# A graph network's prologue, reordered: the samples, the first window's indices and their transposes put ahead of the later layernorm chunks

## The chip, the cores and the metric

The kernel runs on one core of one Trainium2 chip. The metric is the device time of one execution in microseconds (us), the median over several runs. The five engines are named as in the profile: PE (TensorE; PEld is its weight load), DVE (VectorE), ACT (ScalarE), POOL (GpSimd) and SP (SyncE, which here issues transfers).

## The reference

Two message-passing layers on a graph of 6250 nodes with 64 features and 206250 directed edges (`src`, `dst`, sorted by `dst`). Each layer normalizes, aggregates over the edges, applies small dense layers, and is added to its input.

```python
h = jnp.maximum(_layernorm(x, axis=-1), 0.0)
x = x + gin(h)          # twice: h + segment_sum(h[src], dst), then relu(. @ Wa + ba) @ Wb + bb
h = jnp.maximum(_layernorm(x, axis=-1), 0.0)
x = x + message_net(h)  # y = mlp3(h[src]); z = segment_sum(y, dst); mlp3(concat([h, z]))
return x
```

## The kernel before

Instead of gathering per edge, the kernel builds the count matrix A (6250 by 6250, how many edges go from node to node) in 49 row tiles of 128 nodes and multiplies by it. A tile's counts are products of one-hot matrices. A is written to memory as bytes and read twice later, by two sweeps that make up the later part of the run; the first aggregation (`FirstSum`) uses each tile while it is still on chip.

**Finding the edges.** The edges of 256 nodes (a pair of tiles, number `q`) lie in a row in `dst`, so their start must be found. A sample of every 550th entry is loaded (`smp_i`), spread by a product with ones over all partitions (`smp_f`, `smp_d`, `smp`), and `search` counts on ACT with a Sign and an accumulated sum how many samples lie below a node; VectorE turns the count into `row` and `base` (L307, L308). `fetch_blocks` has GpSimd gather the block of 550 (`blk`, L316); `search_block` counts inside it (L327); `fetch_edges` makes the offsets (`off_f`, `off`, L336, L337) and has GpSimd gather the two index windows `d_win` and `s_win` (L341), 128 edges for each pair of nodes. All this goes in batches: batch 0 has one pair of tiles, the others two.

**From indices to counts.** `slots` turns a batch's windows on VectorE into three numbers per edge (L364 to L380); `cast` copies two of them on ACT to bf16; `turn` transposes the three on TensorE (L394) and copies them on ACT to `lkw` (L396). `hot` makes a tile's one-hots on VectorE: `there` (L405), `high` (L409) and `low` (L412); tile 0's come in three pieces (16, 16, 32), all other tiles' in one. `build` runs 64 small products per tile in four groups of 16 (L428), and ACT copies each group to int16 (`a`, L430). After each group a callback `between` runs: a quarter of the sum of the tile before (`FirstSum.quarter`, L571) and what the table `beside` holds for that place, slots, casts, turns, searches and fetches of later batches among them.

**The layernorm.** `values(t)` normalizes a chunk of 7 row tiles (`XT`; there are 7 chunks, 0 to 6). `norm` has VectorE sum (`mean`, L230), scale (L231), subtract (`xm`, L233), ACT square (`sq`, L235), VectorE sum the squares (`var`, L237), ACT take the root (L238), VectorE the reciprocal (L239) and the product `h` (L240). `split` then cuts `h` into three bf16 parts for the exact sum: ACT copies the first (L247), and two times TensorE subtracts what is there (an f32 product L250, one or two bf16 products L252) into the same pair of PSUM buffers `cnt` that the counts use, and ACT copies the rest (L253). The sum of tile 0 needs all seven chunks.

**What sets the order.** The instructions of an engine stand in an order that the framework's scheduler makes from the program's order, its data dependences and its own estimates. `behind(op, other)` adds an order without a semaphore: on the same engine `op` comes after `other`. Every engine works its list off in order, and a wait holds up all that stands behind it. Two buffers of one-hots (`hots`) and two pairs of `cnt` are in turn. In the program before, chunks 0 to 4, the searches of batches 0 to 3 and the fetches of batches 0 to 2 are written ahead of `build(0)`, chunks 5 and 6 behind it; chunks 0 and 1 are tied behind the samples. x is loaded in seven transfers, in turn on SP and ACT (`load_x`), SP's behind the samples.

Of the kernel before, what the change touches and what calls it, by code (L numbers as in the profile page):

```python
# [141 lines left out]
def load_x(nc, xs, x, engines):  # L142
    full = N // P
    nc.vector.memset(xs[:, full, :], 0.0)
    for i, t in enumerate(range(0, full, XT)):
        n = min(XT, full - t)
        engines[i % len(engines)].dma_start(xs[:, t:t + n, :], x[t * P:(t + n) * P].rearrange("(t p) d -> p t d", p=P))
    engines[0].dma_start(xs[:N - full * P, full, :], x[full * P:])


@with_exitstack
def fast(ctx: ExitStack, tc: tile.TileContext, x, src, dst, w, bad, out):
# [13 lines left out]
    def bank(name, dtype=FP):  # L166
        return pmix.tile([P, CH * 4 // mybir.dt.size(dtype)], dtype, tag="mix", name=name)


    root = const.tile([P, 1], FP, name="root")  # L170
# [4 lines left out]
    xs = const.tile([P, NT, D], FP, name="xs")  # L175
    load_x(nc, xs, x, [nc.sync, nc.scalar])
    w.load(nc.sync)
# [10 lines left out]
    ident_a = const.tile([P, P], BF, name="ident_a")  # L188
    nc.vector.tensor_scalar(ident_a, w.ident, 1.0 / UNIT, None, op0=OP.mult)
    word2 = once.tile([P, W, 2], BF, name="word2")  # L190
# [10 lines left out]
    smp_f = once.tile([SP_ROWS, SP_COLS], FP, name="smp_f")  # L201
    nc.vector.tensor_copy(smp_f, smp_i)
    nc.vector.memset(smp_f[0:1, 0:1], -1.0)
# [22 lines left out]
    def norm(to, t, n):  # L226

        xt = xs[:, t:t + n, :]
        mean = work.tile([P, n], FP, name="mean", tag=f"mean{n}")
        begun = nc.vector.tensor_reduce(mean, xt, axis=AX.X, op=OP.add)  # L230
        nc.vector.tensor_scalar_mul(mean, mean, 1.0 / D)  # L231
        xm = work.tile([P, n, D], FP, name="xm", tag=f"xm{n}")
        centered = nc.vector.tensor_tensor(xm, xt, mean[:, :, None].to_broadcast([P, n, D]), op=OP.subtract)  # L233
        sq = work.tile([P, n, D], FP, name="sq", tag=f"sq{n}", bufs=1)
        squared = nc.scalar.activation(sq, xm, AF.Square)  # L235
        var = work.tile([P, n], FP, name="var", tag=f"var{n}")
        nc.vector.tensor_reduce(var, sq, axis=AX.X, op=OP.add)  # L237
        nc.scalar.activation(var, var, AF.Sqrt, bias=w.eps, scale=1.0 / D)  # L238
        nc.vector.reciprocal(var, var)  # L239
        nc.vector.scalar_tensor_tensor(to, xm, 0.0, var[:, :, None].to_broadcast([P, n, D]), op0=OP.max, op1=OP.mult)  # L240
        return begun, centered, squared

    def split(parts, h):

        parts = [parts[:, :, i * D:(i + 1) * D] for i in range(NP)]
        banks = pcnt.tile([P, 2, CH], FP, name="cnt")[:, :, :h.shape[1] * D]
        nc.scalar.copy(parts[0], h)  # L247
        for i in range(2):
            ps = banks[:, i].rearrange("p (t d) -> p t d", d=D)
            nc.tensor.matmul(ps, w.ident, h, start=True, stop=False)  # L250
            for k in range(i + 1):
                nc.tensor.matmul(ps, minus, parts[k], start=False, stop=(k == i))  # L252
            nc.scalar.copy(parts[i + 1], ps)  # L253
# [22 lines left out]

    counted, swept = {}, []

    def behind(op, other):

        tc.add_manual_dep(op.ins, other.ins.name,
                          mybir.DependencyInfo(mybir.DependencyClass.NoSync, mybir.DependencyReason.DATA),
                          reason="order on an engine")
        return op

    def follow(op, engine):

        if engine in counted:
            behind(op, counted[engine])
# [57 lines left out]
    def slots(b):  # L347
# [31 lines left out]
        nc.vector.tensor_scalar(byte, byte, float(BYTE[1] - BYTE[0]), float(BYTE[0]), op0=OP.mult, op1=OP.add)  # L379
        nc.vector.tensor_tensor(byte, byte, shift, op=OP.logical_shift_left)  # L380
        numbers[b] = {0: word, 2: byte}
# [6 lines left out]
    def turn(b, i):  # L388
# [4 lines left out]
        for k in range(3):  # L393
            follow(nc.tensor.transpose(ps[:, k * P:(k + 1) * P], parts2[b % 2][:, i, k, :], identb), "PE")  # L394
        lkw = lkws[starts[b] + i] = wins.tile([P, 3, P], BF, name="lkw", bufs=5)
        nc.scalar.copy(lkw.rearrange("p a b -> p (a b)"), ps[:, :3 * P])  # L396

    def hot(lkw, g0, n):

        def of(i):  # L400
# [12 lines left out]
            low.rearrange("p (g i) w -> p g i w", i=2), there.rearrange("p g w i -> p g i w"),  # L413
            of(2)[:, :, :, None].to_broadcast([P, n // 2, 2, W]), op=OP.mult)
        return low.bitcast(F8), high

# [75 lines left out]
    def values(t):  # L492
        h = work.tile([P, XT, D], FP, name="h")
        begun, centered, squared = norm(h, t, XT)
        if t <= XT:
            behind(begun, sampled)
            behind(begun, bounds)
            behind(squared, searched[0])
        if t == XT:
            behind(centered, searched[1])  # L500
        split(hp[:, t:t + XT], h)
# [44 lines left out]
    values(2 * XT)  # L546
    search(2, op)
    fetch_blocks(2)
    values(3 * XT)
    search(3)  # L550
    fetch_blocks(3)
    values(4 * XT)
    for i in range(2):
        search_block(2, i)
    fetch_edges(2)

# [474 lines left out]
```

## Time and profile before

| what | before |
|---|---|
| median of 3 runs | 888.5 us (888.29 to 891.24) |
| profiled execution, its own time | 887.79 us |
| its span, from the first instruction to the last | 885.3 us |
| PE busy, share of the span | 854.7 us, 97% |
| DVE busy | 629.3 us, 71% |
| ACT busy | 570.7 us, 64% |
| chain that ended last, by engine | PE 81%, DVE 7%, DMA 5%, ACT 4% |

The profile is one execution. Its parts are the busy share of each engine in 40 slices of the span (a digit is tenths), the chain of waits followed back from the last instruction, groups of instructions by line, and, from the trace, a timeline (start, length, engine, line, operation, output and inputs, how often; in brackets the idle time before it and what ended that). Times in it are us from the span's start. Instructions of one engine overlap a little, so the time from one start to the next is some 0.07 us less on VectorE than the length shown. An L250 of the program is two rows in the trace.

### The profile page before, as it was taken

The numbers are of one execution on the slowest core, as the hardware profiler recorded it, in microseconds if no ns is written. First come the engines' busy times: TensorE is split into PE (matmuls) and PEld (weight loads), VectorE is DVE, ScalarE is ACT, GpSimd is POOL, SyncE is SP. The second block draws the span as 40 slices with busy tenths as digits, with TensorE's granted clock in tenths as the row PEclk, the third lists the DMA queues.
The fourth block names the chain that finished last, engine by engine and source line by source line (L and its number), as shares of the span: only waits on it lengthen the run. The fifth ranks groups of instructions, "written<-read, shape, count | busy, mean of one in ns | idle before, by whom it ended". The sixth has DMA issues, their size and how long they took to land.

```text
span 885.3 us, 19697 instructions
## 1 busy us (share of the span) xinstructions
PE 854.7 (97%) x8251; PEld 731.4 (83%) x8251; DVE 629.3 (71%) x933; ACT 570.7 (64%) x775; POOL 126.3 (14%) x86
## 2 busy tenths in 40 slices
PE   3899999999999999999999999999999999999996
PEld 1489999999999999887888887888889877776785
DVE  6999999999999998545555454555456767776662
ACT  5876777776777666645555555554545678777773
POOL 4547742424430200000000000000000000000000
PEclk9999999999999999999999999999999999999998
DMA  6335443335443323744544444444435688888881
GB/s 147 112 115 182 158 173 139 136 136 185 148 156 140 124 111 144 208 111 125 131 122 123 129 117 128 124 117 127 122 98 143 168 220 237 227 234 210 235 215 56
DMA packets 192086, 133.57 MB, mean 151 GB/s; under 512 B 34964, under 2 KB 183316, under 8 KB 191988
## 3 DMA queue, kind: packets, MB, share of 16 engines
q1 hardware_dynamic: 185544, 121.19, 46.6%
q0 software_dynamic: 3600, 10.32, 4.3%
q8 instruction: 66, 1.08, 0.5%
q10 hardware_dynamic: 2844, 0.72, 0.4%
q14 instruction: 32, 0.26, 0.1%
HBM read 91.25 MB, written 40.94 MB: 149 GB/s over the span
## 4 chain that ended last, share of the span: by engine, by line
PE 81%; DVE 7%; DMA 5%; ACT 4%; issue 1%; SPq 0%; ACTq 0%; DVEq 0%
PE acc L748 39%; PE acc L571 21%; PE cnt L428 8%; PE ps_t L450 5%; DMA a<-A 4%; PE ps_y L459 3%; ACT ar L741 2%; DVE ar L741 2%; DVE low L412 2%; PE ps_g L489 1%; DVE high L409 1%; PE cnt L250 1%; DVE there L405 1%; ACT t L452 1%; DMA xs<-in_x_dram 1%
## 5 line engine op out<-in xcount | busy, mean ns | idle before, releaser
L741 DVE CAST ar<-a 128x2048 fp32r<-128x2048 uint8 (+1 forms) x200 | 220.2, 1110 | 187.6 <-PE acc L748 153.8
L741 ACT CAST ar<-a 128x2048 fp32r<-128x2048 uint8 (+2 forms) x126 | 232.3, 1846 | 129.3 <-PE acc L748 104.2
L748 PE MATMUL acc<-ar,h2r 128*128 128x512 f32 (+2 forms) x1274 | 297.7, 388 | 0.0
L748 PEld LDWEIGHTS acc<-ar,h2r 128*128 128x128 f32 x1274 | 229.3, 188 | 49.9 <-issue 5.7
L571 PE MATMUL acc<-hp,a 128*128 128x193 bf16 x2401 | 236.8, 247 | 0.4 <-ACT a L430 0.2
L430 ACT ACTIVATE a<-cnt 128x784 int16<-128x784 f32 x196 | 161.0, 822 | 69.9 <-PE cnt L428 69.0
L571 PEld LDWEIGHTS <-a 128*128 128x128 fp8e4 x2401 | 196.7, 98 | 2.8 <-issue 0.8
L748 PE MATMUL acc<-ar,yr 128*128 128x512 f32 (+2 forms) x637 | 157.7, 399 | 0.0
L748 PEld LDWEIGHTS acc<-ar,yr 128*128 128x128 f32 x637 | 115.7, 188 | 32.7 <-issue 10.1
L428 PE MATMUL cnt<-high,low 128*128 128x49 bf16 x3136 | 113.2, 185 | 1.4 <-DVE low L412 1.2
L428 PEld LDWEIGHTS <-low 128*128 128x128 fp8e4 x3136 | 106.5, 96 | 9.2 <-issue 7.0
L412 DVE TENSOR_TENSOR low<-there,lkw 128x2048 int32<-128x2048 bf16 (+2 forms) x51 | 112.2, 2200 | 0.0
L409 DVE TENSOR_TENSOR high<-high,lkw 128x3136 bf16<-128x3136 bf16 (+2 forms) x51 | 87.8, 1722 | 16.0 <-PE cnt L428 15.5
L316 POOL DMA_INDIRECT blk<-in_dst_dram,row x25 | 60.3, 2411 | 97.5 <-DVE base L308 84.5
L405 DVE TENSOR_TENSOR there<-word,lkw 128x2048 bf16<-128x2048 bf16 (+2 forms) x51 | 59.0, 1175 | 0.3 <-ACT lkw L396 0.3
L341 POOL DMA_INDIRECT s_win<-in_src_dram,off x25 | 36.2, 1449 | 7.6 <-issue 7.6
L341 POOL DMA_INDIRECT d_win<-in_dst_dram,off x25 | 27.6, 1104 | 62.6 <-DVE pair L364 48.5
L250 PE MATMUL cnt<-h,ident 128*128 128x448 f32 x28 | 18.5, 766 | 10.7 <-DVE h L240 8.4
L452 ACT ACTIVATE t<-ps_t,d 128x512 f32<-128x512 f32 (+2 forms) x26 | 17.3, 664 | 11.2 <-PE ps_t L450 11.1
L452 ACT ACTIVATE t<-ps_t,c 128x512 f32<-128x512 f32 (+1 forms) x26 | 17.1, 663 | 7.8 <-PE ps_t L450 7.8
L250 PEld LDWEIGHTS cnt<-h,ident 128*128 128x128 f32 x28 | 5.6, 242 | 18.0 <-issue 7.2
L327 ACT ACTIVATE junk<-blk,below_node 128x550 bf16<-128x550 int32 x25 | 18.7, 748 | 1.9 <-DMA blk<-in_dst_dram,row 1.9
(125 smaller groups left out, 613.8 us busy)
## 6 DMA issues: line engine op xcount, KB each, us to landing
a<-A SPq DMA_DIRECT2D x276, 256.0 KB, 3.2
A<-a SPq DMA_DIRECT2D x49, 784.0 KB, 3.3
a<-A SPq DMA_DIRECT2D x24, 192.0 KB, 2.7
a<-A SPq DMA_DIRECT2D x22, 64.0 KB, 2.7
out_dram<-o SPq DMA_DIRECT2D x11, 128.0 KB, 3.1
xs<-in_x_dram ACTq DMA_DIRECT2D x3, 224.0 KB, 6.0
xs<-in_x_dram SPq DMA_DIRECT2D x3, 224.0 KB, 5.9
blk<-in_dst_dram,row POOLq DMA_INDIRECT x25, 5.4
```

The lines of the kernel that those rows point to most:

```text
L316: nc.gpsimd.indirect_dma_start(out=blks[q], out_offset=None, in_=dst.rearrange("(r b) -> r b", b=BLK), in_offset=bass.IndirectOffsetOnAxis ...
L341: nc.gpsimd.indirect_dma_start(out=win[:, i, :], out_offset=None, in_=of.rearrange("(a o) -> a o", o=1), in_offset=bass.IndirectOffsetOnAx ...
L405: nc.vector.tensor_tensor(there, word2[:, None, :, :].to_broadcast(shape), of(0)[:, :, None, :].to_broadcast(shape), op=OP.is_equal)
L409: nc.vector.tensor_tensor(high, high2[:, None, :, :].to_broadcast(shape), of(1)[:, :, None, :].to_broadcast(shape), op=OP.is_equal)
L412: counted["DVE"] = nc.vector.tensor_tensor(low.rearrange("p (g i) w -> p g i w", i=2), there.rearrange("p g w i -> p g i w"), of(2)[:, :, ...
L428: counted["PE"] = nc.tensor.matmul(ps[:, b, j * H:(j + 1) * H], low[:, g, :], high[:, g // 2, :, g % 2], start=True, stop=True)
L430: counted["ACT"] = nc.scalar.activation(a[:, :, k:k + 2 * PG].rearrange("p h (b j) -> p h b j", b=2), ps[:, :, :PG * H].rearrange("p b (j ...
L450: placed(nc.tensor.matmul(ps[:, :n * P], wt, rhs, start=(i == 0), stop=(i == len(terms) - 1)))
L452: nc.scalar.activation(to, ps[:, :n * P], AF.Relu, bias=bias)
L571: nc.tensor.matmul(acc[:, t % 2, :], self.a[:, k, :], hp[:, k], start=(k == 0), stop=False)
L741: widen(ar.rearrange(f"p k t b -> {order}"), a.rearrange(f"p t (k b) -> {order}", b=P))
L748: op = nc.tensor.matmul(acc[:, :n * P], part, ar[:, k - k0].rearrange("p t b -> p (t b)"), start=(k == 0 and i == 0), stop=(k == H - 1 and ...
```

## The change

It changes the order of the prologue and almost none of its work:

- the x transfers change queues: chunks 0, 2, 4 and 6 on ACT, 1, 3 and 5 on SP behind the samples; the last 106 rows stay on SP;
- the copy of the samples on VectorE comes after the four constants made there;
- chunk 0 starts behind the samples, chunk 1 behind the second search; chunk 2's sum of squares, and the starts of chunks 3 and 4, come behind the end of `slots(0)`; chunks 3 and 4 also behind the first and the second piece of tile 0's one-hots;
- the products of `split` come behind the newest transposes of `turn`;
- chunk 3 with the search and block fetch of batch 2 moves into `build(0)`, after its first group of counts; chunk 4 with those of batch 3 after the second; the search in the blocks of batch 2 and its window fetch after the fourth.

```diff
-    engines[0].dma_start(xs[:N - full * P, full, :], x[full * P:])
+    engines[-1].dma_start(xs[:N - full * P, full, :], x[full * P:])
...
-    load_x(nc, xs, x, [nc.sync, nc.scalar])
+    load_x(nc, xs, x, [nc.scalar, nc.sync])
...
-    nc.vector.tensor_scalar(ident_a, w.ident, 1.0 / UNIT, None, op0=OP.mult)
+    constants = nc.vector.tensor_scalar(ident_a, w.ident, 1.0 / UNIT, None, op0=OP.mult)
...
-    nc.vector.tensor_copy(smp_f, smp_i)
+    behind(behind(nc.vector.tensor_copy(smp_f, smp_i), constants), bounds)
...
-            nc.tensor.matmul(ps, w.ident, h, start=True, stop=False)
+            op = nc.tensor.matmul(ps, w.ident, h, start=True, stop=False)
+            if "turn" in counted:
+                behind(op, counted["turn"])
...
-        nc.vector.tensor_tensor(byte, byte, shift, op=OP.logical_shift_left)
+        counted["slots"] = nc.vector.tensor_tensor(byte, byte, shift, op=OP.logical_shift_left)
...
+        firsts.append(counted["DVE"])
...
-        begun, centered, squared = norm(h, t, XT)
-        if t <= XT:
+        begun, centered, squared, summed = norm(h, t, XT)
+        c = t // XT
+        if c == 0:
             behind(begun, sampled)
-            behind(begun, bounds)
             behind(squared, searched[0])
-        if t == XT:
-            behind(centered, searched[1])
+        elif c == 1:
+            behind(begun, searched[1])
+            behind(squared, searched[0])
+        elif c == 2:
+            behind(summed, counted["slots"])
+        elif c < 5:
+            behind(begun, counted["slots"])
+        if c in (3, 4):
+            behind(begun, firsts[c - 3])
         split(hp[:, t:t + XT], h)
...
-    search(2, op)
-    fetch_blocks(2)
-    values(3 * XT)
-    search(3)
-    fetch_blocks(3)
-    values(4 * XT)
-    for i in range(2):
-        search_block(2, i)
-    fetch_edges(2)
+    beside[0] = [(values, (3 * XT,)), (search, (2, op)), (fetch_blocks, (2,))] + beside[0]
+    beside[1] = [(values, (4 * XT,)), (search, (3,)), (fetch_blocks, (3,))] + beside.get(1, [])
+    beside[3] = [(search_block, (2, 0)), (search_block, (2, 1)), (fetch_edges, (2,))] + beside.get(3, [])
```

More of the change, by code (lines that the diff above doesn't have):

```diff
@@ L167, in bank, with behind @@
         return pmix.tile([P, CH * 4 // mybir.dt.size(dtype)], dtype, tag="mix", name=name)
+    def behind(op, other):
+        tc.add_manual_dep(op.ins, other.ins.name,
+                          mybir.DependencyInfo(mybir.DependencyClass.NoSync, mybir.DependencyReason.DATA),
+                          reason="order on an engine")
+        return op
     root = const.tile([P, 1], FP, name="root")
@@ L236, in norm @@
         var = work.tile([P, n], FP, name="var", tag=f"var{n}")
-        nc.vector.tensor_reduce(var, sq, axis=AX.X, op=OP.add)
+        summed = nc.vector.tensor_reduce(var, sq, axis=AX.X, op=OP.add)
         nc.scalar.activation(var, var, AF.Sqrt, bias=w.eps, scale=1.0 / D)
@@ L240, in norm @@
         nc.vector.scalar_tensor_tensor(to, xm, 0.0, var[:, :, None].to_broadcast([P, n, D]), op0=OP.max, op1=OP.mult)
-        return begun, centered, squared
+        return begun, centered, squared, summed
     def split(parts, h):
@@ L275, in tiles_of @@
         return range(starts[b], starts[b] + BATCHES[b]), slice(starts[b], starts[b] + BATCHES[b])
[L277 to L284, printed above, removed]
+    counted, firsts, swept = {}, [], []
     def follow(op, engine):
@@ L393, in turn @@
         for k in range(3):
-            follow(nc.tensor.transpose(ps[:, k * P:(k + 1) * P], parts2[b % 2][:, i, k, :], identb), "PE")
+            op = nc.tensor.transpose(ps[:, k * P:(k + 1) * P], parts2[b % 2][:, i, k, :], identb)
+            follow(op, "PE")
+        counted["turn"] = op
         lkw = lkws[starts[b] + i] = wins.tile([P, 3, P], BF, name="lkw", bufs=5)
```

## The prediction, made before the changed kernel ran

> **What bounds the kernel now.** I read the busy slices first, then the chain of waits up to 130 us, the table of stretches, the waits by engine, and the timeline where the prologue ends.
>
> ```profile
> PE   3899999999999999999999999999999999999996
> DVE  6999999999999998545555454555456767776662
> ```
> TensorE is full from the third slice on; VectorE is full up to 310 us too. The change touches only the first 55 us, so what counts is how late TensorE's dense stretch begins.
>
> ```profile
> 7.00:27.00 20.00, 11.81 (x22) 4.13 (x22) 15.72 (x52) 13.71 (x37) 10.94 (x10) 1.00 0.51 120
> 27.00:34.00 7.00, 5.25 (x30) 2.13 (x29) 6.85 (x26) 6.69 (x18) 4.21 (x5) 1.00 0.55 162
> 34.00:40.00 6.00, 3.76 (x56) 2.60 (x57) 6.00 (x10) 4.88 (x11) 4.91 (x3) 0.97 0.13 36
> 40.00:53.30 13.30, 12.94 (x147) 9.09 (x146) 12.62 (x21) 9.63 (x22) 7.26 (x4) 0.89 0.23 81
> 84.20:120.00 35.80, 35.76 (x646) 34.57 (x647) 34.28 (x44) 26.67 (x49) 18.40 (x8) 1.00 0.43 161
> ```
> Columns: length, busy PE, weight loads, DVE, ACT, POOL, TensorE clock. VectorE idles 4.3 us before 27 and then works 25.5 of 26.3 us up to 53.3: there its time is the scarce one. From 84 TensorE never waits.
>
> ```profile
> 9.96 0.15 DVE row L307
> 10.17 0.53 DVE xm L233
> 10.70 0.53 DVE var L237
> 27.15 0.43 DVE there L405
> 81.92 2.21 DVE low L412
> 84.18 0.59 PE cnt L428 x16
> ```
> On the chain: the first row number at 9.96, the first one-hot at 27.15, and the last time that TensorE waits for a one-hot.
>
> ```profile
> 12.91 1.83 PE L250 MATMUL cnt<-h,ident 128*128 128x448 f32 x2 [5.69 <-DVE h L240]
> ...
> 32.31 1.02 PE L250 MATMUL cnt<-h,ident 128*128 128x448 f32 x2 [0.82 <-DVE h L240]
> ...
> 41.06 2.29 DVE L412 TENSOR_TENSOR low<-there,lkw 128x2048 int32<-128x2048 bf16 x1
> 46.23 0.63 DVE L240 SCALAR_TENSOR_TENSOR h<-xm,var 128x448 f32<-128x448 f32 x1
> 47.01 0.98 PE L250 MATMUL cnt<-h,ident 128*128 128x448 f32 x2
> 48.03 0.57 PE L428 MATMUL cnt<-high,low 128*128 128x49 bf16 x16
> ```
> The timeline: tile 1's one-hots are ready at 43.35, but its counts start at 48.03, because chunk 6's product (L250) stands in front on TensorE and waits for `h` of chunk 6 (46.86). So two things set the start of the dense stretch: `h` of chunk 6, and then VectorE's one-hots.
>
> **The change, part by part.** Which instruction stands behind which is read from the order of the two built programs, which holds no times; every time is a row of before.
>
> Lead of the first one-hot. The constants move into the wait before the samples, so `smp_d` starts 0.38 earlier (5.00 to 4.62). The sign count is read out at 8.47, yet its row is made at 9.96, since two chunks' means, which wait for x until 7.31, stand in front; now only chunk 0's mean, scale and subtraction (1.2 us) do, so the row comes at 8.47 - 0.38 + 0.04 = 8.1. Chunk 0's load becomes the first of ACT's queue, and that queue's first load moved at 1.8 to 3.2 in the trace of before, so it is there in time; chunk 1 goes behind the samples on SP, where chunk 0 landed at 7.3, before it is used at 8.3. Row to window fetch took 6.1 (9.96 to 16.07); without the reciprocal between, 5.9: 14.0. The indices then land at 17.3 and 18.9 (19.41, 20.95 before). `slots(0)` took 2.8 from there with three layernorm steps between; without them 1.2 to 1.7: done at 20.1 to 20.6. ACT's copy of the transposes now stands behind chunk 2's copies, whose `h` ends at 21.9: 23.5 against 26.64. The first one-hot starts at 24.0, 3.1 earlier (2 to 4), and its `low` ends at 25.5 instead of 28.66.
>
> What VectorE still owes. Moved behind the first `low`: 4 means and scales (4 x 0.63), 3 subtractions (3 x 0.53), one variance 0.53, reciprocal 0.11, `h` 0.60 and a row 0.15, together 5.5 us. VectorE has no idle time there to hide them. Also `high` of tile 2 (1.70) now stands in front of `h` of chunk 6 in the changed order; before, it stood behind.
>
> New waits, which the trace of before does not show. (a) Chunk 3's variance waits for its Square on ACT, and that stands behind the first copy of counts, which waits for TensorE's first 16 counts, and these for chunk 2's products. At the first row's rate those run from 22.9 to 27.8 (two L250 at 1.83, the L252s behind them 0.6, a copy on ACT 0.5); copy of the counts 0.7, search 0.7, Square 0.6: 30.5 with the hand-overs, while VectorE is through at 28.5. So 2.0; at the second row's rate 0.4. I take 2.0: four passes of L250 took 3.32 at 22.19 and 1.84 only from 26.79, so the slow rate held until 26, whatever the table's 1.00 says. (b) `fetch_edges(2)` waits for `search_block(2)`, now behind tile 0's last copy of counts: 0.7 (0 to 1.5). Gone are two waits of 0.3 each. Queued behind both on VectorE are all later one-hots.
>
> `h` of chunk 6: before, 18.2 after the first `low` (28.66 to 46.86); now 18.2 + 5.5 + 1.7 + 2.7 - 0.6 = 27.5, so 25.5 + 27.5 = 53.0, 6.1 late. Chunk 5's two copies on ACT come just before and add up to 0.5, so tile 1's counts start at 54.2 to 54.7 instead of 48.03: 6.4 late.
>
> Behind it. `low` of tile 2 ends at 55.2 (50.7 before). Batch 2's offsets are ready at 48.5 instead of 32.5, and GpSimd's four window fetches took 6.8 us at 32.88 and 8.2 at 44.88, with 2.4 to the landing: 57.7 to 59.1. VectorE reaches the index work of batch 2 at 55.7, so it waits 2 to 3.4 us, with all one-hots behind it. Tile 3's `low` ended 7.8 after that point (50.88 to 58.72); a `there` of the next tile (1.14) also moves in front of it, less the 0.24 it fills: 66.4 to 67.8. TensorE, 6.4 late, wants it at 65.4, so it is 7.4 to 8.8 late there. The `there` moved ahead is saved at tile 4, and where GpSimd, with VectorE standing still, does its four in 5.3 us (as at 20.49), nothing is added: 6.4. The wait at tile 7 (0.47) goes if TensorE alone is late. At the end: 6.4 - 0.5 = 5.9 to 8.8 - 1.1 = 7.7; I take 7.0.
>
> At nothing: ACT's extra load waits for the samples (4.3) and takes under 0.9, while ACT idles until 7.26 (without that cover, 0.9); the last rows' load stays on SP; SP has one load fewer, and weights are wanted at 53 only. `turn` before the later products orders TensorE as the sum has it. From tile 4 on the orders are the same.
>
> The clock: the stretch from 40 has 0.89, that is 3 us at half speed, worth 1.5, and I leave it so. The Trainium skill ("TensorE: Matmul & The Clock Gate", Part 1) has the clock drop to half after an idle window of about 3.4 us and come back after a busy one. By that rule, which speaks against the change, the thinner TensorE work between 28 and 40 would put chunk 4's products and tile 0's sums at half speed as well; the time by it is that of the third rival, by the row that of the sum.
>
> The profiled execution takes 887.8 (span 885.3, 2.5 around it), 0.7 under the median of 888.5. The sum is 887.8 + 7.0 = 894.8, on the median 895.5. Bounds: without (a)'s 1.6, without a half-speed stretch (1.0 on the path), lower end 5.9: +3.3, or 891.8; with the landings 1 us later and upper terms: +10.5, or 899.0.
>
> **The rivals.** *The lead goes through (faster).* If `h` of chunk 6 is ready before 43.7, the one-hots decide and the 3.1 us of lead, the 0.5 of wait and the 1.5 of slow clock are won: 883.4. For it: one-hots of tiles 1 and 2 now lie ready 4.7 and 2.0 us. Against: VectorE's 25.5 of 26.3 us; moved work has no room.
>
> *Debt without new waits (no change).* Lead 3.1 against 5.5 and 1.7, less 0.6: `h` at 50.3, +3.5 us: 892.0. For it: both waits are mine, not the trace's. Against: ACT is 6.69 of 7 us busy when they would arise.
>
> *A cold TensorE (slower still).* The 34 sums of tile 0 at 0.134 (L571 at 41.90: 10 in 1.34) instead of 0.085 take 1.7 more and chunk 4's products 0.8: 895.5 + 2.4 = 897.9. It decides if half speed lasts past 46. Against: clock 1.00 from 26 to 34 with TensorE 5.25 of 7 busy.
>
> **How the numbers follow.** 0.5% (4.4 us) is about what a measurement of this kernel can tell from no change. The sum 0.63 (891.8 to 899.0, a tenth of it under 892.9), cold TensorE 0.18, debt without waits 0.12 (a quarter over 892.9), lead goes through 0.07 (0.06 beyond 0.5%). Slower by over 0.5%: 0.57 + 0.18 + 0.03 = 0.78; faster 0.06; the rest, 0.16, within. The range 890.5 to 899.5 leaves out the faster case and the top of the slowest.
>
> **What would show it.** The chain would have the first row at 8.1 and the first `there` near 24; VectorE waits of about 2 us on `sq` and on `s_win`; the last L240 of the prologue ending near 53; tile 1's counts near 54.5. Wrong: tile 1's counts before 51, or VectorE without waits after 28. A first one-hot after 26 would make all of it later.

## The result

The changed kernel takes 894.09 us in the median (892.92 to 895.55, 7 runs), the kernel before, run beside it, 890.1 us (888.29 to 891.24, 7 runs). The ratio is 1.0056, with a 95% interval of 1.0042 to 1.0071: 5.0 us more (3.7 to 6.3; the two medians alone stand 4.0 us apart). That is slower, by about half a per cent. The profiled executions stand 6.4 us apart in span (891.7 against 885.3). The prediction was 895.5, in a range of 890.5 to 899.5.

Below, what a line of the kernel before calls L240 is L247 in the changed kernel, L250 is L257, L307 is L309, L336 is L338, L371 is L373, L405 is L409, L412 is L416, L428 is L433, L571 is L577. In the kernels of the experiments some numbers are shifted again by a few lines; the names of the tiles tell what a line does.

The busy slices of the changed kernel:

```profile
PE   4689999999999999999999999999999999999997
DVE  5889999999999998635554555555456766766663
```

Hardly anything is to be seen here but TensorE's second and third slice, 6 and 8 where 8 and 9 stood. The table of stretches (length, busy PE, weight loads, DVE, ACT, POOL, clock, DMA share, GB/s) tells more:

```profile
7.00:27.00 20.00, 11.74 (x41) 4.20 (x40) 11.89 (x41) 12.93 (x33) 8.84 (x9) 1.00 0.51 119
27.00:34.00 7.00, 3.25 (x17) 1.92 (x18) 7.00 (x24) 3.08 (x9) 2.18 (x2) 0.66 0.27 81
34.00:40.00 6.00, 3.00 (x9) 1.08 (x8) 5.06 (x14) 3.99 (x10) 0.59 (x1) 0.78 0.01 2
40.00:53.30 13.30, 10.96 (x89) 6.79 (x87) 12.31 (x19) 10.81 (x27) 6.37 (x6) 0.89 0.35 119
84.20:120.00 35.80, 35.78 (x649) 34.70 (x645) 35.51 (x45) 25.28 (x44) 14.58 (x9) 1.00 0.48 173
```

Between 7 and 27 VectorE did 11.9 us of work instead of 15.7 (ahead of 7 it did 3.8 instead of 1.5), so some of its work stands later than before. Behind 27 it is busy nearly all the time, as before, but for two waits, 0.94 us in the third stretch and 0.99 in the fourth. TensorE stands half idle from 27 to 40, at a lower clock. From 84 on the two kernels are alike.

The timeline of the changed kernel, VectorE:

```profile
8.43 0.15 DVE L309 TENSOR_SCALAR row<-sign 128x1 int32<-128x1 f32 x1 [1.55 <-ACT junk L305]
23.88 0.42 DVE L409 TENSOR_TENSOR there<-word,lkw 128x512 bf16<-128x512 bf16 x1 [1.44 <-ACT lkw L400]
28.50 0.61 DVE L244 TENSOR_REDUCE var<-sq 128x7 f32<-128x448 f32 x1
38.20 0.20 DVE L246 RECIPROCAL var<-var 128x7 f32<-128x7 f32 x1 [0.94 <-ACT var L245]
46.90 0.17 DVE L338 SCALAR_TENSOR_TENSOR off_f<-sign,base 128x2 f32<-128x2 f32 x1 [0.99 <-ACT junk L329]
51.28 0.62 DVE L247 SCALAR_TENSOR_TENSOR h<-xm,var 128x448 f32<-128x448 f32 x1
56.54 0.32 DVE L373 TENSOR_SCALAR high_i<-s_win 128x256 int32<-128x256 int32 x1 [2.17 <-DMA s_win<-in_src_dram,off]
```

and TensorE:

```profile
20.68 1.02 PE L257 MATMUL cnt<-h,ident 128*128 128x448 f32 x2 [0.58 <-ACT hp L262]
30.66 1.83 PE L257 MATMUL cnt<-h,ident 128*128 128x448 f32 x2 [4.50 <-DVE h L247]
41.80 1.54 PE L257 MATMUL cnt<-h,ident 128*128 128x448 f32 x2
45.08 3.08 PE L577 MATMUL acc<-hp,a 128*128 128x193 bf16 x34 [0.76 <-ACT a L435]
53.59 0.58 PE L433 MATMUL cnt<-high,low 128*128 128x49 bf16 x16
65.51 0.59 PE L433 MATMUL cnt<-high,low 128*128 128x49 bf16 x16 [0.80 <-DVE low L416]
```

The lead is there: row at 8.43 (9.96 before), first `there` at 23.88 (27.15). It is lost at `h` of chunk 6, which starts at 51.28 instead of 46.23; so tile 1's counts start at 53.59 instead of 48.03, 5.56 us late, and 0.80 us more is added when TensorE waits for tile 3's `low`.

On the chain of waits, which from 39 to 56 us runs over GpSimd and its fetches, batch 2's windows are a piece of their own, which the kernel before did not have at this place:

```profile
47.94 0.94 POOL d_win L343
49.19 0.95 POOL d_win L343
50.44 0.93 POOL s_win L343
...
52.15 4.37 DMA s_win<-in_src_dram,off
...
63.25 2.21 DVE low L416
65.51 0.59 PE cnt L433 x16
```

### The profile page after: what moved, and what is told of

The parts are those of the page before. It is cut to its first block, busy times and chain, and to the rows that moved or that the text cites. A ratio compares the mean times of both kernels' runs of the same rounds, so it can differ in the third digit from the quotient of the medians.

```text
span 891.7 us, 19693 instructions
## 1 busy us (share of the span) xinstructions
PE 855.3 (96%) x8251; PEld 731.9 (82%) x8251; DVE 630.3 (71%) x933; ACT 570.8 (64%) x775; POOL 116.6 (13%) x86
## 4 chain that ended last, share of the span: by engine, by line
PE 80%; DMA 8%; ACT 5%; DVE 3%; issue 3%; POOL 1%; SPq 0%; ACTq 0%; DVEq 0%; POOLq 0%
PE acc L754 37%; PE acc L577 22%; PE cnt L433 9%; DMA a<-A 6%; PE ps_t L455 5%; ACT ar L747 3%; PE ps_y L464 3%; DVE ar L747 1%; PE ps_g L494 1%; DMA s_win<-in_src_dram,off 1%; PE tf L446 1%; POOL d_win L343 1%; ACT t L457 1%; PE acc L579 0%; DMA smp_i<-in_dst_dram 0%
## 5 line engine op out<-in xcount | busy, mean ns | idle before, releaser
L577 PE MATMUL acc<-hp,a 128*128 128x193 bf16 x2401 | 236.5, 247 | 1.7 <-ACT a L435 0.8
L577 PEld LDWEIGHTS <-a 128*128 128x128 fp8e4 x2401 | 195.9, 97 | 3.3 <-ACT a L435 1.1
L433 PEld LDWEIGHTS <-low 128*128 128x128 fp8e4 x3136 | 107.7, 96 | 10.5 <-issue 8.2
L433 PE MATMUL cnt<-high,low 128*128 128x49 bf16 x3136 | 114.2, 186 | 0.9 <-DVE low L416 0.8
L416 DVE TENSOR_TENSOR low<-there,lkw 128x2048 int32<-128x2048 bf16 (+2 forms) x51 | 112.0, 2196 | 0.0
L413 DVE TENSOR_TENSOR high<-high,lkw 128x3136 bf16<-128x3136 bf16 (+2 forms) x51 | 87.8, 1721 | 16.2 <-PE cnt L433 15.7
L318 POOL DMA_INDIRECT blk<-in_dst_dram,row x25 | 56.3, 2252 | 108.0 <-DVE base L310 99.0
L409 DVE TENSOR_TENSOR there<-word,lkw 128x2048 bf16<-128x2048 bf16 (+2 forms) x51 | 58.9, 1174 | 1.5 <-ACT lkw L400 1.4
L343 POOL DMA_INDIRECT s_win<-in_src_dram,off x25 | 34.0, 1361 | 7.6 <-issue 7.6
L257 PE MATMUL cnt<-h,ident 128*128 128x448 f32 x28 | 19.4, 784 | 15.4 <-DVE h L247 10.2
L343 POOL DMA_INDIRECT d_win<-in_dst_dram,off x25 | 24.1, 963 | 67.7 <-DVE pair L366 53.0
L457 ACT ACTIVATE t<-ps_t,d 128x512 f32<-128x512 f32 (+2 forms) x26 | 17.3, 665 | 11.2 <-PE ps_t L455 11.1
L257 PEld LDWEIGHTS cnt<-h,ident 128*128 128x128 f32 x28 | 5.4, 241 | 21.8 <-issue 10.4
```

The source lines that it names most:

```text
L318: nc.gpsimd.indirect_dma_start(out=blks[q], out_offset=None, in_=dst.rearrange("(r b) -> r b", b=BLK), in_offset=bass.IndirectOffsetOnAxis ...
L343: nc.gpsimd.indirect_dma_start(out=win[:, i, :], out_offset=None, in_=of.rearrange("(a o) -> a o", o=1), in_offset=bass.IndirectOffsetOnAx ...
L409: nc.vector.tensor_tensor(there, word2[:, None, :, :].to_broadcast(shape), of(0)[:, :, None, :].to_broadcast(shape), op=OP.is_equal)
L413: nc.vector.tensor_tensor(high, high2[:, None, :, :].to_broadcast(shape), of(1)[:, :, None, :].to_broadcast(shape), op=OP.is_equal)
L416: counted["DVE"] = nc.vector.tensor_tensor(low.rearrange("p (g i) w -> p g i w", i=2), there.rearrange("p g w i -> p g i w"), of(2)[:, :, ...
L433: counted["PE"] = nc.tensor.matmul(ps[:, b, j * H:(j + 1) * H], low[:, g, :], high[:, g // 2, :, g % 2], start=True, stop=True)
```

## The experiments

The theory under test, the debt theory: VectorE's layernorm work that was moved behind the first one-hots makes `h` of chunk 6 late, and that sets the time. Rivals: batch 2's late windows set it (fetch theory), TensorE's slow clock sets it through ACT, or the new front itself costs something. Every kernel was timed beside the kernel before on the same chip; times are given as (ratio - 1) x 888.5 us above the kernel before, with the interval of the ratio in us. "Changed" stands at +5.0 (3.7 to 6.3).

**The moves undone.** `chunks_back` is the changed kernel with this undone:

```diff
-        elif c < 5:
-            behind(begun, counted["slots"])
-        if c in (3, 4):
-            behind(begun, firsts[c - 3])
...
-    beside[0] = [(values, (3 * XT,)), (search, (2, op)), (fetch_blocks, (2,))] + beside[0]
-    ...
+    search(2, op); fetch_blocks(2); values(3 * XT); search(3); fetch_blocks(3); values(4 * XT)
+    for i in range(2): search_block(2, i)
+    fetch_edges(2)
```

> The changed kernel, but chunks 3 and 4 and the searches and fetches of batches 2 and 3 stand in front of tile 0 again. Debt theory: what was moved behind the first low (5.5 us of VectorE) and batch 2's late fetch are the whole loss; both go, so the time falls by 5 to 7 us against the changed kernel and ends 0 to 2 us below the kernel before, with the last h of the prologue near 45 to 47 and no wait on s_win at tile 3. Rival, the new order of the front itself (x on other queues, samples behind the constants) costs something: it stays 2 us or more above the kernel before.

Measured: 1.0002 (0.9986 to 1.0019), +0.2 us (-1.2 to 1.7). By the runs the whole loss goes with the moves; by the spans 1.55 us of it stay (see the lag, kernel by kernel, below). And nothing is won, though the first `there` still starts at 23.90, 3.25 us ahead of the kernel before: `h` of chunk 6 starts at 47.66, later than the theory had it. VectorE and TensorE of this kernel:

```profile
34.56 0.97 DVE L413 TENSOR_TENSOR high<-high,lkw 128x1568 bf16<-128x1568 bf16 x1 [1.51 <-PE cnt L433]
47.66 0.62 DVE L247 SCALAR_TENSOR_TENSOR h<-xm,var 128x448 f32<-128x448 f32 x1
```

```profile
31.79 1.70 PE L257 MATMUL cnt<-h,ident 128*128 128x448 f32 x2
48.42 1.83 PE L257 MATMUL cnt<-h,ident 128*128 128x448 f32 x2 [2.82 <-DVE h L247]
```

The lead ends in VectorE waiting for TensorE to free the one-hot buffers, behind slow products; and `high` of tile 2 stands ahead of `h` of chunk 6 in this order too. From the end of the first `low` to the end of `h` of chunk 6 VectorE is busy for 20.8 of 22.8 us; in the kernel before it is 17.5 of 18.2.

**The front on the kernel before.** `front_alone` is the kernel before with the x queues swapped, the samples behind the constants and chunk 1 behind the second search:

```diff
-    load_x(nc, xs, x, [nc.sync, nc.scalar])
+    load_x(nc, xs, x, [nc.scalar, nc.sync])
...
+    behind(behind(nc.vector.tensor_copy(smp_f, smp_i), constants), bounds)
...
+        elif t == XT:
+            behind(begun, searched[1])
+            behind(squared, searched[0])
```

> The kernel before with the front of the change alone: x on swapped queues, samples behind the constants, chunk 1 behind the row. Debt theory: the first row comes at 8.4 instead of 9.96, and since nothing is moved behind the first low, what is won goes through in part: first there at 25 to 26 (27.15 before), time 0.5 to 1.5 us below the kernel before. Rival, the lead is taken up by the layernorm chunks that fill the room: first there at 27 and the time that of the kernel before within 0.5 us.

Measured: 1.0024 (1.0011 to 1.0037), +2.1 us. The first `there` starts at 25.84, as the debt theory had it, and the time is worse all the same: neither reading foresaw that. ACT and TensorE of this kernel show where it goes:

```profile
29.93 0.75 ACT L326 ACTIVATE junk<-blk,below_node 128x550 bf16<-128x550 int32 x1 [2.71 <-DMA blk<-in_dst_dram,row]
```

```profile
31.25 3.35 PE L256 MATMUL cnt<-h,ident 128*128 128x448 f32 x4 [3.62 <-ACT hp L259]
```

ACT reaches the search in the blocks of batch 2 before the blocks have landed and stands 2.71 us; the copies of `hp` that TensorE needs stand behind it. In the kernel before ACT came there at 29.91 without a wait:

```profile
29.91 0.76 ACT L327 ACTIVATE junk<-blk,below_node 128x550 bf16<-128x550 int32 x1
```

Work pulled forward met a fetch that had not been pulled forward with it. So the rival is not refuted: `front_alone`, and the 1.55 us of `chunks_back` in the span, say that the new front is not free in these orders. How much of the changed kernel's 5.0 us is the front's was not measured apart.

**The fetch of batch 2 earlier.** Two kernels; the first moves the second search and the window fetch one quarter of tile 0 forward, the next two quarters:

```diff
-    beside[3] = [(search_block, (2, 0)), (search_block, (2, 1)), (fetch_edges, (2,))] + beside.get(3, [])
+    beside[2] = [(search_block, (2, 0)), (search_block, (2, 1)), (fetch_edges, (2,))] + beside.get(2, [])
```

> The changed kernel, with the second search of batch 2 and its fetch behind the third quarter of tile 0 instead of the fourth; high of tile 2 still stands ahead of h of chunk 6. Fetch theory (the one-hots of tile 3 set the end): offsets some 3 us earlier, the 2.2 us wait on s_win and the 1.0 us wait on ACT's search go or shrink to under 0.7, time 1.5 to 2.5 us below the changed kernel. Order theory (h of chunk 6 alone sets the end): only what h of chunk 6 gains counts, 0 to 1 us.

Measured: 1.0098 (1.0072 to 1.0124), +8.7 us: neither theory had it, since the edit did not do what it was made for. GpSimd and VectorE:

```profile
47.61 1.74 POOL L343 DMA_INDIRECT d_win<-in_dst_dram,off  x1 [5.55 <-DVE var L246]
49.65 2.60 POOL L343 DMA_INDIRECT d_win<-in_dst_dram,off  x1 [0.30 <-issue]
52.56 2.66 POOL L343 DMA_INDIRECT s_win<-in_src_dram,off  x1 [0.30 <-DVE h L247]
```

```profile
49.66 1.78 DVE L413 TENSOR_TENSOR high<-high,lkw 128x3136 bf16<-128x3136 bf16 x1
52.12 2.28 DVE L416 TENSOR_TENSOR low<-there,lkw 128x2048 int32<-128x2048 bf16 x1
58.03 0.33 DVE L373 TENSOR_SCALAR high_i<-s_win 128x256 int32<-128x256 int32 x1 [3.42 <-DMA s_win<-in_src_dram,off]
```

The fetch starts 0.3 us earlier (47.61 against 47.94), but its first three issues, which lie beside `there`, `high` and `low`, take 1.74, 2.60 and 2.66 us instead of 0.94, 0.95 and 1.40 (the fourth 0.94 instead of 2.84). The windows come 1.5 us later, VectorE waits 3.42 us, TensorE 1.19 at tile 3.

```diff
-    beside[3] = [(search_block, (2, 0)), (search_block, (2, 1)), (fetch_edges, (2,))] + beside.get(3, [])
+    beside[1] += [(search_block, (2, 0)), (search_block, (2, 1)), (fetch_edges, (2,))]
```

> The changed kernel, with the second search of batch 2 and its fetch behind the second quarter of tile 0; by this high of tile 2 (1.70 us) falls behind h of chunk 6, too. Order theory: h of chunk 6 comes 2 to 2.7 us earlier (49.3 instead of 51.9), tile 1's counts at 51, time 2.5 to 3.5 us below the changed kernel and 1 us or more below the kernel with the third quarter. Fetch theory: the one-hots of tile 3 set the end, and VectorE's sum up to them is the same, so both of these kernels gain the same 1.5 to 2.5 us within 0.5.

Measured: 1.0035 (1.0018 to 1.0052), +3.1 us. That is 1.9 us below the changed kernel, though the intervals overlap; order and fetch are both better: `h` of chunk 6 starts at 50.04 (51.28), tile 1's counts at 52.58 (53.59), the wait on `s_win` ahead of tile 3 is gone, and TensorE waits for nothing there. `h` gained 1.2 us and not the 2 to 2.7 of the order theory; but the samples landed 0.9 us later in this trace (`smp_f` at 5.52, 4.62 in the changed kernel), and counted from the first row `h` gained 2.15. Since its partner went wrong, the pair doesn't tell order and fetch apart; the next kernel does.

**VectorE's order put back.** `after_high` and `both_beside` are one kernel, timed on two chips: the changed kernel with `high` and `low` of tile 2 tied behind `h` of chunk 6, and `there` of tile 3 behind that `high`:

```diff
+        if len(firsts) == 5: behind(there_op, counted["high"])
+        if len(firsts) == 4: behind(high_op, counted["h"]); counted["high"] = high_op
+        if len(firsts) == 4: behind(low_op, counted["h"])
```

> The changed kernel with VectorE's order from h of chunk 6 on put back: h, then high and low of tile 2, then there of tile 3 (the changed kernel has high of tile 2 ahead of h, and there of tile 4 ahead of low of tile 3). Order theory: h of chunk 6 and tile 1's counts come 1.7 us earlier (51.9), and the time falls by as much. Fetch theory: the wait on s_win stays at 2.2 us with the same landing (56.5), tile 3's low gains only the 0.9 us of the there that is no longer ahead of it, and TensorE waits 1.5 us there: time 0.5 to 1.0 us below the changed kernel.

> The changed kernel with VectorE's order from h of chunk 6 on tied as in the kernel before, once more, as the third corner beside the two halves. Both theories: 4 to 6 us above the kernel before; if the two parts of the loss add up, its excess is the sum of those of the two halves; if they lie beside each other (VectorE waits for the windows in the time that the debt would have taken), it is that of the larger half within 1 us.

Measured: 1.0057 (1.0037 to 1.0078) and 1.0050 (1.0032 to 1.0069), +5.1 and +4.4 us, the changed kernel's own time within the intervals. VectorE in the second:

```profile
47.29 0.16 DVE L338 SCALAR_TENSOR_TENSOR off_f<-sign,base 128x2 f32<-128x2 f32 x1 [1.92 <-ACT junk L329]
50.28 0.16 DVE L338 SCALAR_TENSOR_TENSOR off_f<-sign,base 128x2 f32<-128x2 f32 x1 [0.57 <-ACT junk L329]
51.20 0.63 DVE L247 SCALAR_TENSOR_TENSOR h<-xm,var 128x448 f32<-128x448 f32 x1
```

`h` of chunk 6 starts at 51.20 although 1.70 us of `high` are gone from in front of it: the waits on ACT's search have grown instead (0.99 to 1.92, and 0.57 that was not there). That `high` had filled a wait. The wait on `s_win` is gone too in this trace, so the fetch theory fails for it: TensorE does not wait at tile 3, and the time is hardly less.

**The two halves.** Both with the tie of `both_beside`. `search_front` puts the searches and fetches of batches 2 and 3 in front again and leaves chunks 3 and 4 beside tile 0; `chunks_front` does it the other way round:

```diff
+    search(2, op); fetch_blocks(2); search(3); fetch_blocks(3)
+    for i in range(2): search_block(2, i)
+    fetch_edges(2)
+    beside[0] = [(values, (3 * XT,))] + beside[0]
+    beside[1] = [(values, (4 * XT,))] + beside.get(1, [])
```

> Chunks 3 and 4 stay beside tile 0, as in the changed kernel; the searches and fetches of batches 2 and 3 are in front again. VectorE's order from h of chunk 6 on is tied as in the kernel before. Debt theory (VectorE's moved layernorm sets the loss): no wait on s_win at tile 3, but h of chunk 6 still 3 to 4 us late (49.5 to 50.5; 46.86 before), time 2.5 to 4 us above the kernel before. Fetch theory (batch 2's late windows are the loss): time within 1.5 us of the kernel before.

```diff
+    values(3 * XT)
+    values(4 * XT)
+    beside[0] = [(search, (2, op)), (fetch_blocks, (2,))] + beside[0]
+    beside[1] = [(search, (3,)), (fetch_blocks, (3,))] + beside.get(1, [])
```

> The other half: chunks 3 and 4 are in front of tile 0 again; the searches and fetches of batches 2 and 3 stay beside tile 0, as in the changed kernel. VectorE's order from h of chunk 6 on is tied as in the kernel before. Debt theory: h of chunk 6 near 47 to 48, time 0 to 1.5 us above the kernel before. Fetch theory: VectorE reaches batch 2's index work at 51 but its windows still land at 55 to 57, so it waits 4 to 6 us there, tile 3's low ends near 63 to 65 instead of 58.7, and the time is 3.5 to 5.5 us above the kernel before, whatever h of chunk 6 does.

Measured: `search_front` 1.0117 (1.0097 to 1.0137), +10.4 us; `chunks_front` 1.0069 (1.0048 to 1.0089), +6.1 us. Each half is worse than both parts together at either place: +0.2 with both in front (-0.3 with the same tie, `back_high` below), +4.4 with both beside. For `chunks_front` it is the trace that says so (7.1 us late against 4.9, in the table of lags below), since its interval overlaps that of `both_beside`. So the loss isn't a sum of two. ACT and VectorE of `search_front`:

```profile
28.76 0.75 ACT L329 ACTIVATE junk<-blk,below_node 128x550 bf16<-128x550 int32 x1 [3.73 <-DMA blk<-in_dst_dram,row]
```

```profile
31.14 0.16 DVE L338 SCALAR_TENSOR_TENSOR off_f<-sign,base 128x2 f32<-128x2 f32 x1 [3.50 <-ACT junk L329]
```

and of `chunks_front`:

```profile
43.99 0.75 ACT L329 ACTIVATE junk<-blk,below_node 128x550 bf16<-128x550 int32 x1 [3.61 <-DMA blk<-in_dst_dram,row]
```

```profile
45.34 0.62 DVE L244 TENSOR_REDUCE var<-sq 128x7 f32<-128x448 f32 x1 [3.59 <-ACT sq L242]
```

Either way ACT stands some 3.7 us in front of blocks that are still on their way, and VectorE with it. The chunks in front fill the time of the fetches in front; take either away, and the queue behind the search stands still. The debt theory said 2.5 to 4 us and 0 to 1.5 for the two, and both are missed. The fetch theory said within 1.5 us for the first; its 3.5 to 5.5 for the second lie within reach of the interval, but not for its reason, since VectorE does not wait for `s_win` there. What outlives this is the middle of the theory, that the start of the dense stretch sets the time; what makes `h` of chunk 6 late is VectorE's work in one order and a wait on a search in another. From the end of the first `low` to the end of `h` of chunk 6 VectorE waits 7.7 of 30.6 us in `search_front` and 4.8 of 22.9 in `chunks_front`; in the changed kernel it is 2.1 of 26.5.

**Less debt.** The kernel `both_beside` without mean, scale and subtraction for chunks 3 and 4 (2.3 us of VectorE):

```diff
+        if t // XT in (3, 4) and n == XT:
+            squared = nc.scalar.activation(sq, xt, AF.Square)
+            ...                                  # h from xt instead of xm
```

> The changed kernel with VectorE's order from h of chunk 6 on tied as before (so to be set against the kernel both_beside: 4.4 us above the kernel before, h of chunk 6 at 51.2). Left out are the mean, the scale and the subtraction of chunks 3 and 4, which are normalized without them: 2.3 us of VectorE's moved work. Debt theory: h of chunk 6 comes about 2.3 us earlier, near 49, and the time stands 1.5 to 3 us above the kernel before. ACT theory (h of chunk 6 waits for ACT's queue of copies and searches, and VectorE's work only fills its waits): h of chunk 6 comes under 0.8 us earlier, VectorE waits that much longer, time 3.7 to 5 us above the kernel before.

Measured: 1.0016 (0.9990 to 1.0043), +1.4 us (-0.9 to 3.8). VectorE:

```profile
48.48 0.63 DVE L256 SCALAR_TENSOR_TENSOR h<-xm,var 128x448 f32<-128x448 f32 x1
```

`h` of chunk 6 starts 2.7 us earlier than at 51.20, tile 1's counts at 50.28 (53.00). The intervals of the two kernels overlap (-0.9 to 3.8 and 2.8 to 6.1), so it is the trace that decides. That the 2.7 us are so near to the 2.3 of the debt theory is luck. The scheduler also set the means, scales and subtractions of chunks 5 and 6 ahead of the first `low`, so VectorE has 4.6 us less work between the end of that `low` and the end of `h` of chunk 6 (18.5 us instead of 23.1); the first `low` ends 0.9 us later, and VectorE waits 1.0 us more. Less work there makes `h` earlier by far more than the ACT theory allowed (0.8), but the price of the 2.3 us alone is not measured.

**Less TensorE.** The same kernel without the second pass of `split` for chunks 3 and 4:

```diff
+            if i >= passes:                      # 1 for chunks 3 and 4, else 2
+                nc.scalar.copy(parts[i + 1], h)
+                continue
```

> As the kernel both_beside, but without the second pass of TensorE (two L257 and two L261) for chunks 3 and 4; ACT copies h in place of its sum, so ACT has the same work and does not wait for TensorE there. About 2.8 us of TensorE at half speed goes for each of the chunks. ACT theory, fed by the slow clock (ACT's copies wait for TensorE's slow products, and VectorE's waits of 1.9 and 0.6 us on ACT's searches come from that): h of chunk 6 comes 2 to 2.7 us earlier, time 1.5 to 2.5 us above the kernel before. Debt theory: VectorE's own work fills the stretch, h of chunk 6 comes under 0.8 us earlier, time 3.7 us or more above the kernel before.

Measured: 1.0051 (1.0024 to 1.0078), +4.5 us, as `both_beside`. VectorE:

```profile
48.76 0.16 DVE L341 SCALAR_TENSOR_TENSOR off_f<-sign,base 128x2 f32<-128x2 f32 x1 [2.30 <-ACT junk L332]
50.74 0.62 DVE L247 SCALAR_TENSOR_TENSOR h<-xm,var 128x448 f32<-128x448 f32 x1
```

`h` of chunk 6 gains 0.46 us, within what the debt theory allowed (0.8), and nothing counted from the end of the first `low`, with the slow products of these chunks halved. So it is not these products that hold it.

**A warm TensorE.** Ten products without use ahead of the first product of chunks 3 and 4 of the changed kernel:

```diff
+            if warm and i == 0:
+                for _ in range(warm):            # 10 for chunks 3 and 4
+                    nc.tensor.matmul(ps, minus, hp[:, :XT, :D], start=True, stop=True)
```

> The changed kernel with ten extra products of 128x448 bf16 (minus by parts of chunk 0, into a bank that the next product overwrites) ahead of the first product of chunks 3 and 4, so that TensorE is busy while it waited for h. Slow-clock theory (the half speed from 29.4 to 44 us, four pairs of L257 at 1.54 to 1.86 instead of 1.02, lies on the chain to h of chunk 6 and causes VectorE's waits of 0.9 and 1.0 us there): the pairs go back to 1.02, h of chunk 6 comes 1.5 to 2.5 us earlier, time 1.5 to 2.5 us below the changed kernel. Debt theory (VectorE's instructions, not TensorE, fill that stretch): the pairs are faster, h of chunk 6 comes under 0.7 us earlier, time within 0.7 us of the changed kernel.

Measured: 1.0102 (1.0080 to 1.0125), +9.1 us. The time tells nothing, since the order changed too. Three of the four pairs of products take 1.00 to 1.02 us, and `h` of chunk 6 starts at 49.52, 1.8 us earlier; but `high` of tile 2 (1.7 us) now stands behind it, and VectorE's waits from the first `low` to the end of `h` are hardly shorter, 1.9 us instead of 2.1. So the gain is that of the order, and the faster products took next to nothing from the waits. The scheduler also moved `h` of chunk 5 to 48.69 (46.98), TensorE stood 4.1 us there and fell to half speed again:

```profile
49.45 1.83 PE L260 MATMUL cnt<-h,ident 128*128 128x448 f32 x2 [4.10 <-DVE row L312]
```

Tile 1's counts start no earlier (54.84 at the first group that the trace shows). `one_pass` puts the question in another way.

**Both in front, with the order tied.** `chunks_back` with the ties of `both_beside`, the candidate to beat both kernels.

> The kernel with chunks 3 and 4 back in front, and VectorE's order from h of chunk 6 on as in the kernel before (h, then high and low of tile 2, then there of tile 3). If the 1.7 us of high of tile 2 is what ate the lead there: h of chunk 6 at 45.9 (47.66 without this edit, 46.23 in the kernel before), chunk 6's product at full speed since TensorE waits 1 us instead of 2.8 for it, tile 1's counts near 47.7 (50.42; 48.03), time 1 to 2 us below the kernel before. If TensorE's slow stretches at 32 us set it instead: within 0.7 us of the kernel before.

Measured: 0.9997 (0.9980 to 1.0013), -0.3 us. `h` of chunk 6 starts at 48.18, not at 45.9: `row` of a later batch, ahead of it, waits 1.33 us for ACT's search. The samples also landed 1.4 us later in this trace (`smp_f` at 5.84, 4.43 in `chunks_back`). No version was found that is faster than the kernel before.

**The lag, kernel by kernel.** In all traces where TensorE runs without pauses of its own, the lag of the late run follows from tile 1's counts. Column 3 is the lag of these counts behind 48.03, plus TensorE's later waits for a `low`, minus the 0.47 us that the kernel before waited at tile 7. Column 4 is the start of the sixteenth `low` against 117.64.

| kernel | tile 1's counts | sum | sixteenth `low` late by | by the runs |
|---|---|---|---|---|
| `chunks_back` | 50.42 | 2.39 - 0.47 = 1.9 | 1.9 | 0.2 (-1.2 to 1.7) |
| `front_alone` | 50.26 | 2.23 + 0.46 - 0.47 = 2.2 | 2.2 | 2.1 (1.0 to 3.3) |
| `edges_first` | 52.58 | 4.55 - 0.47 = 4.1 | 3.9 | 3.1 (1.6 to 4.6) |
| `both_beside` | 53.00 | 4.97 + 0.39 - 0.47 = 4.9 | 4.9 | 4.4 (2.8 to 6.1) |
| changed | 53.59 | 5.56 + 0.80 - 0.47 = 5.9 | 5.9 | 5.0 (3.7 to 6.3) |
| `edges_sooner` | 54.42 | 6.39 + 1.19 - 0.47 = 7.1 | 7.4 | 8.7 (6.4 to 11.0) |
| `chunks_front` | 55.43 | 7.40 - 0.47 = 6.9 | 7.1 | 6.1 (4.3 to 7.9) |
| `search_front` | 57.91 | 9.88 - 0.47 = 9.4 | 9.9 | 10.4 (8.6 to 12.2) |

Columns 3 and 4 agree within half a microsecond: the start of the dense stretch is carried through to the late tiles whole. The runs follow within their intervals but for `chunks_back`. There the time outside the span is shorter, on average 1.5 us over its 12 runs and 2.7 over the 27 of the kernel before beside it, while the medians of the spans stand 1.55 us apart (887.35 and 885.8), near the 1.9 of the trace. So its late start is carried through as well; why less time lies outside the span was not found.

## Why the prediction was right, and where it was not, step by step

The path that the prediction named is the one that the trace shows: a lead at the first one-hot, lost at `h` of chunk 6, and a wait on batch 2's windows behind it. The time is in the lower half of its range, since the waits were smaller than in the sum.

**The lead.** 3.1 us said, 3.27 measured; first `low` ending at 25.5 said, 25.39 measured. The row came 0.3 us later than said, since the samples landed that much later, and the windows landed at 18.35 and not at 17.3; `slots`, 1 us shorter than in the sum, made up for it. So the near agreement is in part luck, two errors that cancel.

**The debt.** 5.5 us of layernorm and 1.7 of `high` were said to be added between the first `low` and `h` of chunk 6. The stretch from the end of that `low` to the end of that `h`, in the kernel before and in the changed one (columns as above):

```profile
28.66:46.86 18.20, 14.21 (x129) 9.03 (x128) 17.52 (x41) 14.66 (x34) 9.71 (x8) 0.91 0.33 108
```

```profile
25.39:51.90 26.51, 17.05 (x125) 9.78 (x124) 24.43 (x58) 18.22 (x45) 7.99 (x7) 0.81 0.25 81
```

VectorE has 6.9 us more work there (7.2 said) and waits 1.4 us more (2.1 said). That is the sum's own mechanism. `no_means`, with 4.6 us less work than `both_beside`, has `h` 2.7 us earlier. With `chunks_back` half of the added work goes (20.8 us of it are left, 17.5 before), and by the runs the whole loss.

**`high` of tile 2, 1.70 us: there, but not worth its duration.** `both_beside` took it away, and `h` moved by 0.1 us, 0.5 counted from the first row. Behind it stood a wait for ACT's search that it had covered (VectorE waits 3.1 us in the stretch instead of 2.1). The prediction priced the instruction by its duration and did not ask what would be waited for without it.

**Wait (a), 2.0 us: not where it was said.** Chunk 3's sum of squares (28.50) does not wait. The step took TensorE's slow rate to hold until 26, as in the trace of before; in the changed kernel the products run at 1.02 us a pair from 20.68, so the counts and ACT's copies came in time. A wait of its kind comes one chunk later, 0.94 us at 38.20, when the clock had fallen again. **Wait (b)** was said to be 0.7 and is 0.99. Together 1.93 instead of 2.7.

**`h` of chunk 6** was said for 53.0 and ended at 51.90: by the stretches above 0.7 us of this are waits, 0.3 work and 0.1 the first `low`. Tile 1's counts: 54.2 to 54.7 said, 53.59 measured.

**Batch 2's windows.** A wait of 2 to 3.4 us was said, 2.17 measured; tile 3's `low` at 66.4 to 67.8 said, 65.46 measured; TensorE 7.4 to 8.8 late there said, 6.5 measured. The sum said +7.0 at the end; the late tiles are 5.9 late, the runs +5.0. The sum is too large by the 0.8 us that tile 1's counts are less late (5.56, 6.4 said) and by what VectorE's wait adds on top, 0.80 us of TensorE's and not up to 2.4. `both_beside`, without the wait, is 1.0 us less late by the trace, which its runs don't resolve.

**The clock** fell more than the sum allowed. By the granted clock, read in slices of 1 us, TensorE is at half speed from 29.2 to 36.0 and from 39.5 to 42.9 us, 10.2 us in all; in the kernel before it is from 39.6 to 43.0. (The expectation of `warm` took it for one stretch up to 44.) The rival of a cold TensorE needed it past 46 and did not get it: tile 0's 34 sums took 3.08 us, 0.09 each. The Trainium skill ("TensorE: Matmul & The Clock Gate", Part 1) has the clock fall after an idle window of about 3.4 us and rise after a busy one. The changed kernel's trace agrees for the fall (products at 1.83 us behind 4.50 us of idleness). The kernel before does not fit as plainly: its clock fell at 39.6, though TensorE had been busy for 1.5 of the 3.4 us ahead, without a pause above 0.86. Of what the prediction took from the page, chunk 4's products were at half speed (1.58 and 1.54 us a pair), tile 0's sums were not. `one_pass` and `warm` show that the slow products, as far as they take them away, cost `h` of chunk 6 little.

**The lead going through** (7 in 100) failed for the reason that the prediction gave against it, VectorE's 25.5 of 26.3 us. **Debt without new waits** was named as 892.0; the waits are there, but smaller than in the sum, and the measured time lies between the two.

## What to carry to other kernels

An earlier first result is worth something only if the stage behind it has room for the work that was moved: read how busy the scarce engine is after the point, not how idle it is before it. Where engines work their lists in order, a search and the work that fills its fetch belong together: against the kernel before, moving the layernorm chunks alone cost 10 us here, moving the searches and fetches alone 6, moving both 4 to 5. And an instruction in front of the critical one costs its duration only if the engine would not have stood there anyway.

## What the runs showed of the hardware that was not expected

GpSimd's issue of an indirect fetch took 0.94 us in many places and 2.60 and 2.66 us beside VectorE's `high` and `low` in `edges_sooner`, so an earlier start brought the data later. It is not so each time: in the changed kernel an issue at 49.19, beside a `high` from 49.24 on, took 0.95. The Trainium skill ("GPSIMD Engine Reference", section 8, Key points) says that GpSimd shares its memory interfaces with VectorE and contends with some of VectorE's instructions; the slow issues agree with that, the one at 49.19 does not, and no run shows that this is the cause.

The kernel before took 888.2 to 890.1 us in three of the five comparisons and 907.9 and 912.8 us in two, on other chips. One kernel was traced in both kinds, as `both_beside` and as `after_high`. The stretch from 120 to 300 us:

```profile
120.00:300.00 180.00, 179.81 (x3204) 175.08 (x3202) 168.66 (x229) 130.71 (x232) 60.37 (x40) 1.00 0.42 152
```

and in the slower kind, with TensorE's two groups that have the idle time:

```profile
120.00:300.00 180.00, 169.83 (x2939) 162.39 (x2937) 156.56 (x208) 120.71 (x215) 55.83 (x36) 1.00 0.39 141
```

```profile
L584 PE MATMUL acc<-hp,a 128*128 128x193 bf16 x1212 | 119.6, 247 | 4.9 <-ACT a L442 4.7
L440 PE MATMUL cnt<-high,low 128*128 128x49 bf16 x1568 | 59.2, 186 | 5.3 <-issue 5.2
```

At the same clock and the same 247 ns a product, TensorE idles 10.2 of 180 us there, half of it with nothing to wait for that the profile shows. The cause is open; ratios were only taken within one chip. The five kernels timed on such chips (`warm`, `after_high` and `back_high` on one, `no_means` and `one_pass` on the other) are left out of the table of lags for that reason.
